# Seven-for-eight products applied twice to the queries and keys of a decoder layer, over eight tiles at once, with each half of the tokens taken through all heads by itself

## The chip, the cores and the metric

The kernel runs on one core of a Trainium2 chip. The metric is the device time of one execution in microseconds (us); less is better. The kernel before takes 1988.46 us, the median of three runs (1988.45, 1988.46 and 1991.81).

The engines of a core each work through their own list of instructions in order: TensorE (PE, matrix products, with its weight loads listed apart as PEld), VectorE (DVE), ScalarE (ACT), GpSimd (POOL), and SyncE (SP), which here only issues transfers (DMA). TensorE writes its results into PSUM, from where VectorE and ScalarE read them.

## The reference

One decoder layer on 2048 tokens (32 sequences of 64) of 512 features, all in float32. Each of the three blocks takes a layer-normalised input and is added to the residual:

```python
x = x + attn(layernorm(x))                # 32 heads of 128
x = x + xattn(layernorm(x), ctx_1024)     # one head, on the transposed layout
x = x + ffn(layernorm(x))                 # top 8 of 64 experts, each a bias vector

def attn(h):
    q = rmsnorm((h @ Wq + bq).reshape(b, n, 32, 128), gq)
    k = rmsnorm((h @ Wk + bk).reshape(b, n, 32, 128), gk)
    v = (h @ Wv + bv).reshape(b, n, 32, 128)
    p = softmax(einsum('bnhd,bmhd->bhnm', q, k) / sqrt(128))
    return einsum('bhnm,bmhd->bnhd', p, v).reshape(b, n, 4096) @ Wo + bo
```

The change concerns the first block: the products `h @ Wq` and `h @ Wk` (512 x 4096 each), and the order in which heads and tokens are gone through.

## The kernel before, in words

The tokens lie in 16 tiles of 128. Four tiles make a *quad* (512 tokens, `NQUAD` = 4), two heads make a *head group* (`HG` = 2, `NHG` = 16). The attention phase runs 64 steps: for every head group, for every quad (`order`). One step projects the quad to queries, keys and values of two heads, and does the attention of earlier steps in between.

**Seven for eight.** `HeadGroup.project` treats a step's projection as a 2 x 2 block product: two blocks of tokens (even and odd tiles of the quad) and two halves of the 512 features on the left, the same two halves of features and the two heads on the right. Instead of eight block products it makes seven, of sums and differences of blocks. The left sums (`s1` to `s4`) are made once per quad in `AttentionInput.turn`, the right ones (`t1`, `t2`, `t4` and a new `b12`) once per head group in `Weights.sums`, by POOL. Each of the seven is done once for queries and keys (`wide`, L313: four matmuls with 256 columns, j = queries or keys, c = the two 128-row parts of the half) and once for values (`narrow`, L325: four matmuls with 128 columns). A matmul in float32 shows as two records in the trace.

**Accumulating in place.** The seven results are combined in PSUM where possible: `pa` takes products 1, 6, 7 and 4 one on top of the other, and after each it is read out (`p1`, `u2`, `u3`, and the last result) by VectorE before the next is added; `pb` takes 5 and 3; `pc` takes 2. So product 6 may not start before `p1` has been read, 7 not before `u2`, 4 not before `u3`. Between two `wide` products of `pa` other products are placed. The pool `ps_a` has three buffers, for `pa`, `pc` and `pb`. Values do the same in `va` and `vb` with ScalarE copies.

**The attention of earlier steps.** In the step of unit n, `turn_probabilities` transposes the probabilities of unit n-2, `scale` (L472 on POOL for keys, L474 on VectorE for queries) multiplies the inverse root mean squares of unit n-1 in, `mix` makes probabilities times values of unit n-2 (L524), `scores` the products of queries and keys of unit n-1 (L487), `statistics` the sums of squares of unit n (L443, from squares that ScalarE made, L353), `store` copies the mixed values out (L539) and sends them to the scratch tensor `mixed` in HBM, `deviations` computes the inverse roots (ScalarE: a table load and a logarithm, L456, another table load and an exponential, L457), sends 8 KB to `row` in HBM and fetches them back broadcast over all partitions (`rsb`, 1 MB), and `probabilities` starts the softmax (VectorE maximum L235 and difference L236, ScalarE exponential L237). The rest of the softmax (sum L240, reciprocal L242, POOL product L243) and the query scalings wait in a list, `waiting`; after each product `take_waiting` puts one of them on its engine.

**Order.** The order of TensorE's instructions is the program's own everywhere, that of VectorE and ScalarE during the attention phase (`manual_schedule`). POOL's and SP's lists are arranged by a scheduler when the program is built. Weights of the next head group are fetched at quad 0, their sums are made at quads 1 and 2.

**The output phase.** `plain_out` multiplies the first two tiles of `mixed` by Wo, filling TensorE while the last attention steps drain. Then `strassen_out` does seven for eight for each further pair of tiles, with right sums from `wo_sums`, and `after_attention` runs cross-attention and experts for each tile. Constants for these (`bo_b`, `xw`, `rwt`, `rb_b`, `eb_sb`) are loaded early, in `load_constants`.

## Time and profile before

| what | us |
|---|---|
| median of three runs | 1988.46 |
| the profiled execution | 1986.83 |
| its span, first to last instruction | 1985.0 |
| TensorE busy (matmuls) | 1943.9 |
| VectorE / ScalarE / POOL busy | 963.1 / 722.0 / 526.4 |
| mean granted TensorE clock | 0.994 |
| `wide` products (L313), all matmul groups together | 856.4 |
| data moved | 185.25 MB |

A group's line gives the source line, the engine, the operation, the tiles written and read, their shapes and the count; then busy time, the mean duration of one in ns, and the idle time of the engine just before such instructions with what ended it. A line of the timeline gives the start in us from the span's start, the duration, the engine, the line, the operation, the tiles, and in brackets the engine's idle time before it. Durations of matmuls overlap, since they are pipelined; the pitch from one start to the next is the time they take.

The steady part of the attention phase is periodic: `wide` product 1 of one step starts at 805.89, that of the next at 828.04 and that of the one after at 850.18, so a step takes 22.14 us.

### The profile page before, as it was taken

The page shows a single profiled execution, that of the slowest core. Times are in us where ns is not written, and L with a number is a line of the kernel's source. Part 1 is how long each engine was busy: PE and PEld are TensorE (multiplying, and loading weights), DVE is VectorE, ACT ScalarE, POOL GpSimd, SP SyncE. Part 2 cuts the span into 40 slices and gives each one's busy share as a digit, 9 for nine tenths or more (in the row PEclk, how much of TensorE's full clock was granted, in tenths as well). Part 3 has the DMA queues.
Part 4 walks back from the last instruction along what each step waited for, and adds up shares of the span by engine and source line. Part 5 has one row for each costly group of instructions (what it writes and reads, how often), then busy time and mean ns, then how long its engine had stood idle before and what let it go on. Part 6 is the DMA issues. An engine that isn't in the chain of part 4 may idle for free.

```text
span 1985.0 us, 40265 instructions
## 1 busy us (share of the span) xinstructions
PE 1943.9 (98%) x17269; PEld 1699.8 (86%) x17269; DVE 963.1 (49%) x1766; ACT 722.0 (36%) x1499; POOL 526.4 (27%) x563
## 2 busy tenths in 40 slices
PE   6899999999999999999999999999999999999997
PEld 6788888888888888888888888888888888888875
DVE  5544444444444444444444444444453455544554
ACT  2343444444444444444444443444321112221112
POOL 4333322313132221313131232211123133331320
PEclk9999999999999999999999999999999999999997
DMA  4232222312232232223232232226423321233100
GB/s 129 93 103 98 97 100 74 118 65 97 76 118 78 84 107 87 97 66 107 82 102 97 76 108 76 97 74 193 163 94 143 109 90 62 67 109 109 43 24 21
DMA packets 126785, 185.25 MB, mean 93 GB/s; under 512 B 7312, under 2 KB 107728, under 8 KB 114320
## 3 DMA queue, kind: packets, MB, share of 16 engines
q1 hardware_dynamic: 125424, 181.61, 27.0%
q8 instruction: 136, 2.23, 0.5%
q10 hardware_dynamic: 1184, 1.08, 0.2%
q14 instruction: 41, 0.34, 0.1%
HBM read 144.39 MB, written 38.27 MB: 92 GB/s over the span
## 4 chain that ended last, share of the span: by engine, by line
PE 95%; DVE 2%; issue 1%; POOL 1%; ACT 1%; DMA 0%; POOLq 0%; DVEq 0%; ACTq 0%
PE pa L313 22%; PE py L581 19%; PE va L325 11%; PE pb L313 11%; PE vb L325 8%; PE pc L313 5%; PE o L524 4%; PE s L487 3%; PE ms L443 3%; PE pt_p L227 1%; PE py_x L793 1%; PE e_x L756 1%; PE pt_x L227 1%; PE py_x L791 1%; PE pl_f L812 1%
## 5 line engine op out<-in xcount | busy, mean ns | idle before, releaser
L353 ACT ACTIVATE sq<-qk 128x512 f32<-128x512 f32 x256 | 161.8, 632 | 610.3 <-DVE qk L350 610.3
L581 PE MATMUL py<-wo,a 128*128 128x256 f32 x1152 | 262.3, 381 | 0.0
L243 POOL TENSOR_TENSOR prob<-prob,inv 128x512 f32<-128x512 f32 x64 | 66.9, 1046 | 718.0 <-DVE inv L242 718.0
L472 POOL TENSOR_TENSOR qk<-qk,rsb 128x256 f32<-128x256 f32 x256 | 182.0, 743 | 261.5 <-DMA rsb<-row 261.5
L313 PE MATMUL pa<-xc,w 128*128 128x256 f32 x1024 | 249.7, 387 | 0.0
L313 PE MATMUL pa<-xc,t 128*128 128x256 f32 x1024 | 242.5, 380 | 6.5 <-DVE u L404 6.5
L581 PEld LDWEIGHTS py<-wo,a 128*128 128x128 f32 x1152 | 214.1, 190 | 37.3 <-issue 9.0
L313 PEld LDWEIGHTS pa<-xc,w 128*128 128x128 f32 x1024 | 185.3, 191 | 46.2 <-issue 25.9
L313 PEld LDWEIGHTS pa<-xc,t 128*128 128x128 f32 x1024 | 184.8, 190 | 26.7 <-DVE u L404 6.9
L581 PE MATMUL py<-wo_t,a 128*128 128x256 f32 x608 | 140.6, 381 | 0.0
L325 PEld LDWEIGHTS va<-t,xc 128*128 128x128 f32 x1024 | 134.4, 192 | 6.6
L539 ACT ACTIVATE ot<-o,bvt 128x256 f32<-128x256 f32 x256 | 100.6, 476 | 105.4 <-PE o L524 105.4
L325 PE MATMUL vb<-w,xc 128*128 128x128 f32 x1024 | 135.1, 275 | 0.0
L325 PE MATMUL va<-w,xc 128*128 128x128 f32 x1024 | 135.1, 275 | 0.0
L325 PE MATMUL va<-t,xc 128*128 128x128 f32 x1024 | 134.9, 275 | 0.0
L325 PEld LDWEIGHTS vb<-w,xc 128*128 128x128 f32 x1024 | 129.5, 192 | 3.3
L325 PEld LDWEIGHTS va<-w,xc 128*128 128x128 f32 x1024 | 129.5, 192 | 3.3
L474 DVE SCALAR_TENSOR_TENSOR qk<-qk,gqk,rsb 128x256 f32<-128x256 f32 x256 | 127.3, 498 | 0.0
L581 PEld LDWEIGHTS py<-wo_t,a 128*128 128x128 f32 x608 | 113.0, 190 | 14.8
L313 PE MATMUL pb<-xc,t 128*128 128x256 f32 x512 | 122.1, 382 | 0.0
L313 PE MATMUL pc<-xc,w 128*128 128x256 f32 x512 | 121.1, 379 | 0.0
L313 PE MATMUL pb<-xc,w 128*128 128x256 f32 x512 | 121.0, 379 | 0.0
(165 smaller groups left out, 2806.6 us busy)
## 6 DMA issues: line engine op xcount, KB each, us to landing
rsb<-row SPq DMA_DIRECT2D x64, 1024.0 KB
mixed<-ot SPq DMA_DIRECT2D x64, 512.0 KB
a<-mixed SPq DMA_DIRECT2D x32, 1024.0 KB
x<-in_x_dram SPq DMA_DIRECT2D x32, 256.0 KB
w<-in_wq_dram SPq DMA_DIRECT2D x32, 256.0 KB
wo<-in_wo_dram SPq DMA_DIRECT2D x8, 1024.0 KB
w<-in_wk_dram SPq DMA_DIRECT2D x30, 256.0 KB
w<-in_wv_dram SPq DMA_DIRECT2D x30, 256.0 KB
```

Of the source, the lines that this page charges most:

```text
L227: nc.tensor.transpose(pt[:, j, :], src[:, j, :], ident)
L243: nc.gpsimd.tensor_tensor(prob, prob, _bc(inv, k), ALU.mult)
L313: nc.tensor.matmul(to[:, j, :], right[i][:, c, j, :], left[i][:, c, :, :].rearrange("p j n -> p (j n)"), start=first and j == 0 and c == 0 ...
L325: nc.tensor.matmul(to[:, j, :], left[i][:, c, j, :], right[i][:, c, 2, :], start=first and j == 0 and c == 0, stop=c == 1, skip_group_chec ...
L353: nc.scalar.activation(sq, it, AF.Square)
L443: nc.tensor.matmul(ms[rows, ab, :], ones, self.sq[h, ab][:, j, :], start=True, stop=True,)
L472: nc.gpsimd.tensor_tensor(k, k, self.rs[:, 2 * h + 1, ab, :], ALU.mult)
L474: lambda q=q, rs=self.rs[:, 2 * h, ab, :]: nc.vector.scalar_tensor_tensor(q, q, gqk, rs, ALU.mult, ALU.mult)
L487: nc.tensor.matmul(s[h * SEQ : (h + 1) * SEQ, i, b, :], qk[:, 0, tok], qk[:, 1, tok], start=True, stop=True,)
L524: nc.tensor.matmul(o[b][dims, h, i, :], self.v[h, i % 2][rows, i // 2, dims], probt[rows, i, h * SEQ : (h + 1) * SEQ], start=True, stop=True,)
L539: nc.scalar.activation(ot[:, h, :, b * SEQ : (b + 1) * SEQ], o[b][:, h, :, :], AF.Identity, bias=bvt[:, hg * HG + h : hg * HG + h + 1],)
L581: nc.tensor.matmul(py, a[:, g, :], b[g // KH][:, g % KH, :], start=n == 0 and g == 0, stop=n == last and g == NHG - 1,)
```

## The change

For head groups 1 to 15 two quads are now projected at once (`Window`, eight tiles, 1024 tokens). Each of the seven outer products for queries and keys has the shape (256 features) x (two quads' blocks of 256 columns) x (queries and keys), and is itself done as a 2 x 2 block product with seven instead of eight: seven matmuls of 128 x 128 weights on 256 columns. Left sums of the second level are made by `inner_inputs` once per half of the tokens, right ones by `more_sums` once per use of a head group's weights, on POOL. Values stay at one level. Head group 0 runs as before, quad by quad (`single`).

The loop order changes: all 16 head groups for the first half of the tokens, then all 16 for the second half, so each group's weights are fetched and summed twice. The steady unit is a window of one head group and two quads, of which there are 30; there are four single steps.

```diff
+        def outer(self, o, to, add=None, bias=None):
+            left, right = halves_x[self.half, o], self.w.inner[o]
...
+            def product(i, bank, first=True):
+                nc.tensor.matmul(
+                    bank, right[i], left[i], start=first, stop=True, skip_group_check=True
+                )
+
+            def read(bank, t, j, out):
+                b = None if bias is None else bqk[:, j, bias : bias + 1]
+                if add is not None and b is not None:
+                    nc.vector.scalar_tensor_tensor(
+                        out, bank, b, add[t][:, j, :], ALU.add, ALU.add
+                    )
+                elif add is not None:
+                    nc.vector.tensor_tensor(out, bank, add[t][:, j, :], ALU.add)
+                elif b is not None:
+                    nc.scalar.activation(out, bank, AF.Identity, bias=b)
+                else:
+                    nc.scalar.copy(out, bank)
...
+            pa = bank("pa")
+            product(1, pa)
+            p1 = part("p1", "p1")
+            read(pa, 0, 0, p1)
+            pc = bank("pc")
+            product(2, pc)
+            nc.vector.tensor_tensor(to[0][:, 0, :], pc, p1, ALU.add)
+            pb = bank("pb")
+            product(5, pb)
+            product(6, pa, first=False)
+            u2 = part("u2", "u2")
+            read(pa, 0, 1, u2)
+            yield
+            product(7, pa, first=False)
+            u3 = part("u3", "p1")
+            read(pa, 1, 1, u3)
+            nc.vector.tensor_tensor(to[1][:, 1, :], pb, u3, ALU.add)
+            yield
+            product(4, pa, first=False)
+            read(pa, 1, 0, to[1][:, 0, :])
+            product(3, pb, first=False)
+            nc.vector.tensor_tensor(to[0][:, 1, :], pb, u2, ALU.add)
+            take_waiting()
```

At each of the two `yield`s of an outer product, `run` puts one product of the values (`self.v()`) and then whatever is listed for that place (o, n); place (o, 2) is after the outer product:

```diff
+            c11 = tiles(0, 0)
+            run(1, c11)
+            place(1, 2)
+            c12 = tiles(1, 0)
+            run(6, c12, c11)
+            place(6, 2)
+            c21 = tiles(0, 1)
+            run(7, c21, c12)
+            place(7, 2)
+            c22 = tiles(1, 1)
+            run(5, c22, None, heads[1])
+            for t in range(2):
+                nc.gpsimd.tensor_tensor(c12[t], c12[t], c22[t], ALU.add)
+            for t in range(2):
+                nc.gpsimd.tensor_tensor(c22[t], c22[t], c21[t], ALU.add)
+            place(5, 2)
+            run(2, c11, c11, heads[0])
+            squares(1, 1)
+            squares(0, 0)
+            place(2, 2)
+            run(4, c21, c21, heads[0])
+            squares(0, 1)
+            run(3, c12, c12)
+            squares(1, 0)
+            place(3, 2)
...
+        places = {
+            (6, 1): line.turn,
+            (6, 2): line.scale,
+            (7, 2): line.scale,
+            (5, 2): line.scale,
+            (2, 2): lambda: attend(0),
+            (4, 1): line.scale,
+            (3, 1): line.turn,
+            (3, 2): end,
+        }
```

`attend` does for one unit what the end of a step did: `mix`, `scores`, the sums of squares, `store`, the inverse roots and `probabilities`, in this order; it comes twice in a window, after outer product 2 and after outer product 3, which is the window's last. The sums of squares of a window are taken in two parts, first of (head 0, even tiles) and (head 1, odd tiles), then of the other two. `Line.scale` does half of a unit's scaling at a time, four times in a window, from a fetch of 512 KB:

```diff
-            self.rs = work.tile([P, 2 * HG, 2, QT], F32, tag="rsb", name=f"rsb_{name}", bufs=1)
...
+            self.rs = work.tile(
+                [P, 2, 2, QT], F32, tag="rsb", name=f"rs{part}_{self.name}", bufs=1
+            )
```

The weights of a group and all their sums lie in one of two 32 KB blocks (`four_blocks`), the seven left blocks of a half of the tokens in a pool of seven 8 KB blocks. In the last window the loads of Wo take over these blocks (`wo_0` and `a_0` early, the second column half of Wo after the window's products), and `drain` interleaves the last attention work with `plain_out`. The constants of the output phase are now loaded after the attention phase's pool is closed:

```diff
+    bo_b = work.tile([P, D], F32, tag="bo", name="bo_b", bufs=1)
+    load(bo_b, bo.partition_broadcast(P))
+
+    xw = work.tile([P, 4, P], F32, tag="xw", name="xw", bufs=1)
+    nc.gpsimd.memset(xw, 0.0)
+    for j, src in enumerate((xwq_t, xwk_t, xwv_t, xws_t)):
+        for b in range(2):
+            half = slice(b * SEQ, (b + 1) * SEQ)
+            load(xw[half, j, half], src)
...
     pt = ps_t.tile([P, 2, P], F32, tag="pt", name="pt_xw")
     for j in range(2):
         nc.tensor.transpose(pt[:, j, :], xw[:, j, :], ident)
```

The sums of the second level, and the order of groups:

```diff
+        def more_sums(self):
...
+                nc.gpsimd.tensor_tensor(t1, b12, b11, ALU.subtract)
+                nc.gpsimd.tensor_tensor(t2, b22, t1, ALU.subtract)
+                nc.gpsimd.tensor_tensor(t4, b21, t2, ALU.subtract)
+                nc.gpsimd.tensor_tensor(b12, b22, b12, ALU.subtract)
...
-    order = [(hg, quad) for hg in range(NHG) for quad in range(NQUAD)]
...
+    groups = [(hg, half) for half in range(2) for hg in range(NHG)]
```

## The prediction

> **What bounds the kernel now.** First the busy shares and the chain of work that ended last:

> ```profile
> PE 1943.9 (98%) x17269; PEld 1699.8 (86%) x17269; DVE 963.1 (49%) x1766; ACT 722.0 (36%) x1499; POOL 526.4 (27%) x563
> ...
> PE 95%; DVE 2%; issue 1%; POOL 1%; ACT 1%; DMA 0%; POOLq 0%; DVEq 0%; ACTq 0%
> ```

> TensorE sets the time, and nearly nothing holds it up. So a matmul removed is worth its pitch, and a wait added is worth its length. Why TensorE never waits is seen in the timeline of one step boundary:

> ```profile
> 802.71 1.16 PE L524 MATMUL o<-probt,v 64*64 64x64 f32 x64
> 803.91 1.57 ACT L539 ACTIVATE ot<-o,bvt 128x256 f32<-128x256 f32 x4 [1.25 <-PE o L524]
> 804.89 1.07 PE L443 MATMUL ms<-sq,ones 128*32 128x256 f32 x16
> 805.89 1.99 PE L313 MATMUL pa<-xc,w 128*128 128x256 f32 x8
> 806.07 1.28 ACT L456 ACT_TABLE_LOAD   x1 [0.59 <-PE ms L443]
> 807.92 0.69 DVE L368 TENSOR_TENSOR p<-pa,bqk 128x512 f32<-128x512 f32 x1 [1.43 <-PE pa L313]
> 809.90 0.62 ACT L237 ACTIVATE prob<-prob 128x512 f32<-128x512 f32 x1
> 810.42 0.35 ACT L374 COPY v<-va 128x256 f32<-128x256 f32 x1
> 810.55 0.69 DVE L240 TENSOR_REDUCE sums<-prob 128x8 f32<-128x512 f32 x1 [1.94 <-ACT prob L237]
> 811.23 1.89 PE L313 MATMUL pa<-xc,t 128*128 128x256 f32 x8
> ```

> After `ms` ScalarE needs until 810.52, 4.63 us after TensorE went on at 805.89, for two table loads and three activations; the value copy L374 stands behind them, and VectorE waits there too (L240). TensorE doesn't notice: the next read of `pa` (L368) is VectorE's and comes first, and product 6, which needs it, starts only at 811.23, after two wide (1.73 each) and two narrow products (0.89). Third, what a late read costs:

> ```profile
> 60.70 1.99 PE L313 MATMUL pa<-xc,t 128*128 128x256 f32 x8 [3.30 <-DVE u L404]
> 62.53 1.04 PE L227 MATMUL pt_a<-ident,x 128*128 128x128 f32 x8
> ...
> 1961.05 1.09 PE L227 MATMUL pt_f<-ident,xn_f 128*128 128x128 f32 x4 [3.71 <-DVE inv_x L782]
> ```

> The read L404 ended at 60.64, the matmul began at 60.70: 0.06 us to release it. A wide product after a wait has a pitch of 1.83 instead of 1.73: 0.1 for the restart. From the groups, the durations for the new shapes:

> ```profile
> L361 DVE TENSOR_TENSOR v<-vb,w 128x256 f32<-128x256 f32 x128 | 54.3, 424 | 74.0 <-PE vb L325 42.1 <-ACT w L413 31.6
> L395 ACT COPY w<-va 128x256 f32<-128x256 f32 x64 | 23.9, 373 | 85.0 <-PE va L325 85.0
> L125 POOL TENSOR_TENSOR t<-w,t 128x768 f32<-128x768 f32 x31 | 56.5, 1822 | 5.5 <-DMA w<-in_wv_dram 5.4
> ```

> **What goes.** A window replaces two steps (44.28 us). Its queries and keys take 49 matmuls of 256 columns instead of 56; a wide product of four takes 1.73, so one takes 0.432, and seven are 3.02 us per window. Values, mix, scores, sums of squares and transposes keep their counts. Over 30 windows 91 us: the whole possible gain.

> **What covers shrink.** A product on `pa` is now one matmul, 0.432, not four. A reader starts 0.20 us after the pitch of its product ends (L368: 807.92 against 807.72), takes 0.36 (ScalarE) or 0.42 (VectorE), and releases after 0.06. I follow one window:

> *First outer product after `attend(1)`.* It adds nothing and has no bias, so its reads are ScalarE copies, and in ScalarE's order they stand behind `store`, both table loads and the exponential. Read 0.36 and 0.05 more after 4.63, release 0.06: product 6 at 5.10 after `ms`; products 1, 2 and 5 cover 1.30. Wait 3.8. I take 3.4, because `ms` itself ends 0.45 later (below) while ScalarE's chain, which starts with `store`, moves less. Bounds 2.9 and 3.8. Behind the waiting copy on ScalarE stand the reads for `u2`, `u3` and the value copies, and TensorE behind all of them.

> *First outer product after `attend(0)`* (outer 4). Here VectorE reads, but `take_waiting` puts the softmax sum between `u2` and `u3`, and it waits for the exponential: 4.63 + 0.03 + 0.92 (sum and reciprocal) + 0.47 (read with two additions, by L474's 498 ns and L361's 424) + 0.06 = 6.11; product 4 is due after 4 x 0.432 + 0.89 + 0.432 + 0.89 = 3.94. That is 2.2; 1.9 with `ms` late. Bounds 1.2 and 3.0.

> *Sums of squares.* After outer 2 ScalarE has four squares (632 ns each), after outer 3 two, where before one was left; `store` follows them, and `ms` waits for the PSUM buffer that the first half of `store` frees (the same three buffers go round). Squares of (1,1) also need POOL's two additions of `c22`. I get 0.8 and 0.5, together 1.3; bounds 0.5 and 1.6.

> *From one outer product to the next.* Product 1 reuses `pa`, read last after product 4; only product 3 covers: 0.20 + 0.42 + 0.06 - 0.43 = 0.25, up to 0.43 where a query scaling (0.48) or the copy `probt` (0.69) is ahead in VectorE's queue. Five of these, with small waits for `u3` and the value copies, 2.0. Bounds 1.0 (if a read of 256 takes half of 512's 692) and 3.0.

> *Restarts.* Some 13 waits per window, 0.1 each: 1.3; bounds 0.8 and 1.5.

> Sum per window: -3.02 + 3.4 + 1.9 + 1.3 + 2.0 + 1.3 = +6.9, so 51.2 instead of 44.28; 30 windows +207. The bounds together give +3.4 to +9.9.

> **What I cost at nothing, and its cover.** POOL per window, in us: four sums of 768 (1.82), sums and additions of 512 (eight, 1.25, between L243's 1046 ns and the 1308 of the residual sum) and 384 (four, 1.0, between 743 at 256 and 1046), eight scalings (0.73), two products (1.04): 29 of 51. If its queue slipped by 3 us the squares would slip with it. VectorE gets 41 operations at 0.42 for 14 at 0.69: +7.5, some 29 of 51. The weights fetched twice add 25 MB; SP issues six transfers of about 0.47 us at the window's start, 1.57 MB at the 350 GB/s seen in the stretch of the Wo loads are 4.5 us, and the sums have until the window's end. The inverse roots come in four fetches of 512 KB, each only when POOL and VectorE have used the one before: in the rows 1 MB took 4.7 us from issue (811.83) to use (816.51), of which 3 are the data, so 3.2 here; outer products are five to six apart, which covers it. At 4.7 the query scaling would block VectorE in outers 5 and 2: +1.8 per window.

> **The clock.** The gap at the window's start is as long as the gaps at which rows begin to differ: after 3.30 the clock stayed (granted 1.00 there), after 3.71 it fell (0.51 from 1960 to 1970). A cold restart costs about 1.0 (the wide product at 29.65 took 2.90 for 1.89). I take a fall in five windows, +5 us; bounds 0 and 30. [...]

> **Once.** In the drain VectorE's list has four Wo sums ahead of the softmax end that `pt_p` needs after one chunk of `plain_out`. They wait for four loads of 1 MB that can start only as the last window frees its blocks, about 2 us before its products end: 1 + 4 x 3.0 + 1.5 (a fetch between) later, then 2.3 for the last sum, 2 for sum, reciprocal and POOL: TensorE is ready at 5.6 after the products, the probabilities at 18: 12 us; bounds 0 and 15. At the start of `strassen_out` the transposes of `xw` wait for its memset, which POOL has behind two sums of 2048 (4.52 each), then for SP's 11 issues and a 1 MB load of `a12`: 8.5; bounds 0 and 15. The second half's first inputs are turned with only `attend` as cover: 2. The four single steps otherwise cost what the first four cost before. Together 23.

> Against the profiled execution: 1986.8 + 207 + 5 + 23 = 2222. The runs' median is 1.6 above that execution, within what can be told.

> **Rivals.** *The waits are covered* and the removed matmuls come out: 1986.8 - 91 + 23 = 1919. The place is product 6 of a window's first outer product; it decides whether its ScalarE read is done 1.30 us after `ms`, or all waits sum to under 3.02. For it: VectorE and ScalarE are under half busy. Against it: L374 at 810.42 shows a copy queued behind the exponential. 3%. *Shorter waits*: reads of 256 near 0.35, `store` not pushed back: +3.4 per window, 1986.8 + 102 + 10 = 2099. For it: the reads of 512 take 0.61 in pitch. 15%. *Late fetches and a cold clock*: +1.8 for late inverse roots and a fall in every window, 1986.8 + 30 x 8.7 + 30 + 23 = 2301. For it: fetches share the queue with the weights, and rows of a fetch during the Wo loads show `row` taking 2.8 instead of 1.8 us. Against it: three of the four fetches come after the weights are in. 12%. My forecast has 70%, 2150 to 2270 by itself.

> The range, 2105 to 2300, leaves out the first rival and the ends of the others. About 4 us (0.2%) is what a measurement can tell from no change. Faster 3%, same 1%, slower 96%.

> **What would show it.** Windows of about 51 us; TensorE waiting 3 to 4 us at product 6 of outer product 1, once per window, for ScalarE; 1 to 3 us in outer 4 for VectorE's `u3`; many waits of 0.2 to 0.4 on the reads of `pa`. Matmuls of 256 columns fewer by 420 records. Wrong would be: windows at 41 to 43 us, or waits mostly for POOL or transfers, or a slow clock throughout.

## The result and the profile after

| | before | after |
|---|---|---|
| median of four runs, us | 1988.45 | 2329.30 |
| lowest and highest, us | 1987.30, 1991.81 | 2323.36, 2341.39 |
| profiled execution, us | 1986.83 | 2323.36 |

The changed kernel takes 1.172 times as long, 95% interval 1.167 to 1.177. The direction was as forecast; the time, 2329, lies 29 us above the upper end of the range. The profiled executions differ by 336.5 us where the forecast had 235.

The page of the changed kernel, busy shares and chain of waits:

```profile
PE 1989.6 (86%) x16849; PEld 1652.8 (71%) x16849; DVE 1271.8 (55%) x2604; ACT 815.9 (35%) x1739; POOL 1099.7 (47%) x1015
...
PE 50%; DVE 17%; ACT 16%; DMA 10%; POOL 3%; issue 3%; SPq 0%; ACTq 0%; POOLq 0%; DVEq 0%
```

The 420 matmul records are gone (17269 to 16849), so the change does what it says. TensorE's share of the chain fell from 95% to 50%; VectorE, ScalarE and transfers have the rest. Here is what TensorE waited for in all (total, times, longest):

```profile
PE pa_w L622 <- ACT p_w L637: 100.5, 30, 3.5
PE pa_w L622 <- DVE u_w L629: 92.3, 58, 3.1
PE pt_a L234 <- DVE x L272: 23.7, 4, 12.9
PE ms_w L720 <- ACT ot L577: 21.7, 56, 0.6
PE pa L414 <- DVE u L461: 14.3, 3, 11.0
PE pa_w L622 <- DVE u_w L633: 13.1, 26, 0.9
PE pb_w L622 <- DVE qk L658: 12.8, 26, 1.3
PE pt_p L234 <- POOL prob L250: 8.4, 1, 8.4
```

The first line is product 6 behind ScalarE, once in each of the 30 windows, 3.35 us on average; the second is `u3` behind VectorE, twice in a window (53.3 us in outer product 4 and 39.0 in outer product 2). Both stand in a window's timeline, here from the last `ms` of one window on:

```profile
1059.19 1.07 PE L720 MATMUL ms_w<-sq,ones 128*32 128x256 f32 x16 [0.32 <-ACT ot L577]
1060.19 0.70 PE L622 MATMUL pa_w<-x,w 128*128 128x256 f32 x2
1060.37 1.28 ACT L589 ACT_TABLE_LOAD   x1 [0.50 <-PE ms_w L720]
1061.15 0.59 PE L622 MATMUL pb_w<-x,w 128*128 128x256 f32 x2
1064.20 0.61 ACT L244 ACTIVATE prob<-prob 128x512 f32<-128x512 f32 x1
1064.72 0.35 ACT L637 COPY p_w<-pa_w 128x256 f32<-128x256 f32 x1
1065.12 1.22 PE L622 MATMUL pa_w<-x,w 128*128 128x256 f32 x2 [3.37 <-ACT p_w L637]
1066.14 1.91 PE L353 MATMUL va<-w,x 128*128 128x128 f32 x8
1067.84 1.06 PE L622 MATMUL pa_w<-x,w 128*128 128x256 f32 x2
1068.70 1.91 PE L353 MATMUL vb<-w,x 128*128 128x128 f32 x8
1070.40 0.99 PE L622 MATMUL pa_w<-x,w 128*128 128x256 f32 x2
```

(Each single product has two records here, `x2`: 840 products on `pa_w` and 1680 records.) The copy of `p1` comes last on ScalarE, at 1064.72, and TensorE stands from 1061.75 to 1065.12. Behind the gap it is slow: a value product takes 1.91 where it takes 1.05 elsewhere, a single product 1.06 for 0.60. Such rows follow 26 of the 30 gaps.

The time from this product 6 to that of the next window is 53.2 us in the first half of the tokens and 53.3 in the second (14 periods from 960.34 to 1707.07 are 746.7), where two steps took 44.28 and the forecast had 51.2. So the windows cost 30 x 9.0 = 270 us, and some 66 us lie outside them.

### The profile page after: what moved, and what is told of

It reads as the page before. It is cut to its first block, busy times and chain, and to the rows that moved or that the text cites. A ratio compares the mean times of both kernels' runs of the same rounds, so it can differ in the third digit from the quotient of the medians.

```text
span 2321.6 us, 41752 instructions
## 1 busy us (share of the span) xinstructions
PE 1989.6 (86%) x16849; PEld 1652.8 (71%) x16849; DVE 1271.8 (55%) x2604; ACT 815.9 (35%) x1739; POOL 1099.7 (47%) x1015
## 4 chain that ended last, share of the span: by engine, by line
PE 50%; DVE 17%; ACT 16%; DMA 10%; POOL 3%; issue 3%; SPq 0%; ACTq 0%; POOLq 0%; DVEq 0%
PE py L767 16%; PE pa_w L622 10%; DMA rs<-row_w 8%; PE va L353 6%; DVE qk L512 6%; PE pb_w L622 4%; ACT L589 3%; PE vb L353 3%; ACT L590 3%; PE ms_w L720 3%; PE pc_w L622 2%; ACT ot L577 2%; DVE qk L658 2%; ACT sq L325 2%; ACT rs_w L589 2%
## 5 line engine op out<-in xcount | busy, mean ns | idle before, releaser
L622 PE MATMUL pa_w<-x,w 128*128 128x256 f32 x1680 | 547.1, 409 | 210.0 <-ACT p_w L637 100.5
L622 PEld LDWEIGHTS pa_w<-x,w 128*128 128x128 f32 x1680 | 283.7, 199 | 297.2 <-ACT p_w L637 112.6
L510 POOL TENSOR_TENSOR qk<-qk,rs 128x256 f32<-128x256 f32 x256 | 196.5, 788 | 499.6 <-DMA rs<-row_w 481.8
L353 PEld LDWEIGHTS va<-w,x 128*128 128x128 f32 x2048 | 286.3, 204 | 28.2 <-ACT w L394 14.5
L353 PE MATMUL va<-w,x 128*128 128x128 f32 x2048 | 293.4, 290 | 2.4 <-ACT w L394 0.4
L120 POOL TENSOR_TENSOR w<-w 128x768 f32<-128x768 f32 x126 | 225.9, 1815 | 111.0 <-DMA w<-in_wv_dram 105.7
L622 PE MATMUL pb_w<-x,w 128*128 128x256 f32 x840 | 256.0, 386 | 14.0 <-DVE qk L658 12.8
L325 ACT ACTIVATE sq<-qk 128x512 f32<-128x512 f32 x256 | 147.8, 623 | 287.8 <-DVE qk L663 205.3
L353 PEld LDWEIGHTS vb<-w,x 128*128 128x128 f32 x1536 | 219.0, 206 | 12.6
L353 PE MATMUL vb<-w,x 128*128 128x128 f32 x1536 | 218.3, 289 | 0.0
L512 DVE SCALAR_TENSOR_TENSOR qk<-qk,gqk,rs 128x256 f32<-128x256 f32 x256 | 189.2, 741 | 25.1 <-DMA rs<-row_w 22.6
L633 DVE TENSOR_TENSOR u_w<-pa_w,qk 128x256 f32<-128x256 f32 x180 | 76.1, 423 | 72.9 <-PE pa_w L622 72.9
```

Of the source, the lines that this page charges most:

```text
L120: on.tensor_tensor(*(it.rearrange("p c j d -> p (c j) d") for it in (out, a, b)), ALU.subtract)
L325: nc.scalar.activation(sq, of, AF.Square)
L353: nc.tensor.matmul(to[:, j, :], left[i][:, c, j, :], right[i][:, c, 2, :], start=first and j == 0 and c == 0, stop=c == 1, skip_group_chec ...
L510: nc.gpsimd.tensor_tensor(k, k, rk, ALU.mult)
L512: lambda q=q, rq=rq: nc.vector.scalar_tensor_tensor(q, q, gqk, rq, ALU.mult, ALU.mult)
L622: nc.tensor.matmul(bank, right[i], left[i], start=first, stop=True, skip_group_check=True)
```

## Experiments

Each kernel is the changed one with the edit shown; times are medians and are set against 2329. The kernel before, run beside them, had 1990.6 to 1993.3, so differences under about 10 us are not read.

**First outer product read on VectorE**

```
-                    nc.scalar.copy(out, bank)
+                    nc.vector.tensor_copy(out, bank)
```

> The first outer product of a window is read on VectorE instead of ScalarE; nothing else. Theory (ScalarE's queue): product 6's wait of 3.37 us per window goes, because its operand no longer stands behind store, two table loads and the exponential; VectorE's softmax sum then holds u3 as in outer product 4 (1.77 us), so 1.6 us per window come back, 48 us, and another 1.2 us per window, 36 us, if the matmuls after that gap were slow because of it: about 2245 us. Rival (the wait only moves: ScalarE's value copies behind the same chain stop TensorE just as long): 2310 to 2330 us.

Measured 2234.5 us, 95 less (ratio to before 1.122, interval 1.120 to 1.124). TensorE's waits in this run:

```profile
PE pa_w L622 <- DVE u_w L629: 97.6, 58, 3.0
PE pa_w L622 <- DVE u_w L637: 48.8, 29, 1.7
PE ms_w L720 <- ACT ot L577: 22.8, 55, 2.3
```

ScalarE's line is gone; in its place `u3` of the first outer product (L637) waits 1.7 us for the softmax sum ahead of it in VectorE's list, as it does in outer product 4. The theory holds, the part about the matmuls behind the gap included: 48 us alone would have given 2281. TensorE's busy time falls from 1989.6 to 1938.4 us for the same 16849 records.

**The gap filled with matmuls**

```
             product(5, pb)
+            if o == 1:
+                for _ in range(7):
+                    product(5, pb)
             product(6, pa, first=False)
```

> In the first outer product of each window product 5 is computed eight times instead of once (same operands, same place), 7 x 0.43 = 3.0 us of matmuls in the gap before product 6, which can start no earlier than before; the wait left is 0.4 us. Theory (the idle gap makes the clock fall): the matmuls after the gap take 0.43 us again, 1.0 to 1.5 us less per window, 30 to 45 us in all, 2285 to 2300 us, and the granted clock of the windows is near 1.00. Rival (those matmuls are slow for another reason, or the clock falls for another reason): 2325 to 2335 us.

Measured 2282.6 us, 47 less (1.146, interval 1.143 to 1.148) with 210 matmuls more. Two stretches, first of the changed kernel and then of this run (busy time of TensorE, its weight loads, VectorE, ScalarE, POOL; then the granted clock, the DMA share and GB/s):

```profile
200.00:400.00 200.00, 170.99 (x1714) 141.45 (x1712) 116.33 (x249) 85.00 (x159) 107.36 (x98) 0.97 0.29 92
1200.00:1400.00 200.00, 169.70 (x1686) 141.30 (x1686) 111.27 (x239) 85.42 (x159) 103.71 (x93) 0.94 0.28 91
```

```profile
200.00:400.00 200.00, 178.10 (x1776) 148.11 (x1777) 119.16 (x250) 89.04 (x166) 109.73 (x100) 1.00 0.30 96
1200.00:1400.00 200.00, 177.32 (x1691) 148.00 (x1690) 121.02 (x255) 83.27 (x158) 114.44 (x101) 1.00 0.27 85
```

Product 6 can start no earlier, yet each window is 1.6 us shorter by the medians (1.2 to 1.4 in the two profiled executions): the clock stays at 1.00. So the idle gap of 3.4 us is followed by a lower clock in nearly every window (26 of the 30 of the changed kernel), which costs 1.2 to 1.6 us beside the gap itself.

**Softmax end one place later, and the softmax's exponential first**

```
             next(it)
+            waiting.append(lambda: None)
             waiting.append(lambda: next(it, None))
```

> The softmax sum, reciprocal and normalization are taken by VectorE and POOL one place later, behind u3 and its addition. Theory (VectorE's list): the wait of 1.77 us for u3 in outer product 4 goes, 30 x 1.77 = 53 us, about 2277 us; in the first outer product the wait for ScalarE stays. Rival (it is only pushed on: product 4 waits for its read behind the same sum, or the transposes of the probabilities wait for POOL): 2315 to 2340 us.

Measured 2320.6 us, 9 less (1.165, interval 1.163 to 1.167), which is too little to read. The waits for `u3` do fall, from 92.3 to 37.7 us. In the last stage one group's probabilities are turned before they are normalized here. The rival: product 2 of the next outer product now waits, 32.0 us in 30 times, for the read that stands behind the sum. A second edit takes the cause away instead:

```
-            if deviations:
-                deviations()
             if self.before:
                 self.before.probabilities()
+            if deviations:
+                deviations()
```

> In attend the softmax's exponential is put ahead of the logarithm and exponential of the inverse roots on ScalarE, with both table loads behind it; nothing else. Theory (the softmax sum in VectorE's list waits for an exponential that is third in ScalarE's chain): the exponential is done some 2.5 us sooner, u3 in outer product 4 no longer waits, 30 x 1.77 = 53 us less, about 2276 us; product 6 of the first outer product still waits 3.4 us, since its read stands behind the same chain. Rival (as in the run before, the wait is pushed on to the next read): 2310 to 2330 us.

Measured 2283.7 us, 46 less (1.147, interval 1.143 to 1.151):

```profile
PE pa_w L622 <- ACT p_w L637: 105.6, 30, 3.6
PE pa_w L622 <- DVE u_w L629: 37.8, 28, 2.9
```

Of the 58 waits for `u3`, those of outer product 4 are gone and the 28 of outer product 2 stay; ScalarE's are 5 us longer. What was late was the exponential, third in ScalarE's chain.

**Two fetches of inverse roots for one**

```
-            self.rs = work.tile(... tag="rsb", bufs=1)
-            nc.sync.dma_start(out=self.rs ..., in_=self.row[part] ...)
+            for h in range(HG):
+                rs = work.tile([P, 2, QT], F32, tag=f"rsb{h}", ...)
+                nc.sync.dma_start(out=rs, in_=self.row[part][:, h, :].partition_broadcast(P))
```

> Each fetch of inverse roots, 512 KB for two heads, becomes two of 256 KB into buffers of their own, so that the first head's starts as soon as its scalings are done. Theory (VectorE's query scaling waits for the fetch and holds u3 in outer product 2, 1.4 us per window): half to all of it goes, 25 to 45 us, 2285 to 2305 us. Rival (VectorE is late there for its own work, the fetch is hidden): 2325 to 2335 us.

Measured 2282.0 us, 47 less (1.145, interval 1.143 to 1.147); the waits for `u3` of outer products 4 and 2 (L629 before the edit) fall from 92.3 to 68.3 us, all of it in outer product 2 (39.0 to 15.0), and the waits for `pb` in outer product 5 (12.8) are gone. That is just above the theory's upper end. So the time of the fetch decides most of this wait, though POOL's work is the same; how it does so is seen next.

**What TensorE waits for in outer product 2.** The changed kernel's timeline there:

```profile
1036.08 2.48 POOL L702 TENSOR_TENSOR qk<-qk,qk 128x512 f32<-128x512 f32 x2
1037.32 1.53 DVE L512 SCALAR_TENSOR_TENSOR qk<-qk,gqk,rs 128x256 f32<-128x256 f32 x1 [0.25 <-DMA rs<-row_w]
1038.77 0.47 DVE L629 SCALAR_TENSOR_TENSOR u_w<-pa_w,bqk,qk 128x256 f32<-128x256 f32 x1
1039.30 0.70 PE L622 MATMUL pa_w<-x,w 128*128 128x256 f32 x2 [1.44 <-DVE u_w L629]
```

The query scaling waits 0.25 us for its fetch and then takes 1.53 us, where it mostly took 0.48 before; `u3` stands behind it. All its records between 200 and 700 us, parted by whether a POOL instruction ran at its start or began within 0.06 us of it:

| us on VectorE | alone | beside POOL, mean (longest) |
|---|---|---|
| query scaling, before (L474) | 0.48 (74 records) | 0.57 (0.97), 17 records |
| query scaling, after (L512) | 0.48 (20) | 0.87 (1.52), 58 |
| read of `pa` with an addition, after (L633) | 0.42 (42) | 0.42 (0.43), 71 |

The scaling reads two operands from SBUF; L633 reads one from PSUM and is not touched. How long a scaling lasts follows from POOL: of the 110 in this trace that start with more than 0.25 us of a POOL instruction still to run, every one ends 0.27 to 0.30 us behind that instruction. Over the 30 windows VectorE is idle for the fetch 0.44 us on average ahead of the scaling in outer product 2, the scaling takes 1.22 and TensorE waits 1.30. With two fetches it was 0.01, 0.92 and 0.50: a scaling that starts sooner finds less of POOL's work beside it. Three runs were to show what this is worth.

```
-                waiting.append(lambda ...: nc.vector.scalar_tensor_tensor(q, q, gqk, rq, ...))
+                nc.gpsimd.tensor_tensor(q, q, rq, ALU.mult)
```

> The changed kernel with the scaling of the queries on POOL, behind that of the keys, instead of on VectorE; the common gain of queries and keys is left out. Theory (VectorE's query scalings, which wait for the fetch and are stretched while POOL works, 0.87 us on average against 0.48 with POOL idle, hold u3 in outer products 2 and 5): those waits, 1.4 and 0.45 us per window, and some restarts go, 50 to 65 us less: about 2270 us, although POOL has 5.9 us more to do per window. Rival (POOL's list is what is late; more work there makes it later): 2330 to 2370 us.

Measured 2572.8 us, 244 more (1.291, interval 1.288 to 1.293):

```profile
PE ms_w L716 <- ACT ot L573: 331.0, 57, 14.9
PE pa_w L618 <- ACT p_w L633: 101.4, 30, 3.5
...
PE pa_w L618 <- DVE u_w L625: 19.2, 23, 1.8
```

The waits for `u3` do go (92.3 to 19.2), but the rival is right in kind, and its 2330 to 2370 far too low: POOL's four scalings now wait for each fetch, the sums of `c12` and `c22` stand behind them, the squares behind those, and `ms` waits 11 us per window. POOL is busy 49% of the span only; it is the order in its list that counts.

```
-                nc.gpsimd.tensor_tensor(t1, b12, b11, ALU.subtract)
...
+                    4: r[:, 1, 0, :],
+                    5: r[:, 0, 1, :],
+                    6: r[:, 1, 1, :],
```

> The changed kernel without the second-level sums of the weights (eight subtractions on POOL per window, 9 us); the products of the second level read first-level parts in their place, so matmuls keep count and shape. Theory (POOL's work stretches VectorE's scalings and delays the fetches behind its own): 15 to 35 us less, 2295 to 2315 us, and the scalings in outer product 5 take 0.5 us. Rival (POOL is covered, as the forecast had it): 2325 to 2332 us.

Measured 2266.3 us, 63 less (1.137, interval 1.134 to 1.140), twice what was expected: the waits at L633 (13.1 us; this is outer product 7, the expectations call it 5) are gone and those at the kernel's start are shorter (23.7 to 15.5, 14.3 to 6.5), but outer product 2 still waits 1.3 us on average, since the pair sums run there, not these. The other half of the 63 us is no wait at all: for the same 16849 records TensorE is busy 32 us less, at a granted clock of 0.976 for 0.956. The gap before product 6 is as long as ever (3.38 us), but here it is followed by a fall of the clock in 14 windows, in the changed kernel in 26; the last section shows on what that hangs.

```
-            for t in range(2):
-                nc.gpsimd.tensor_tensor(c12[t], c12[t], c22[t], ALU.add)
-            for t in range(2):
-                nc.gpsimd.tensor_tensor(c22[t], c22[t], c21[t], ALU.add)
```

> The changed kernel without POOL's four additions on the queries and keys behind outer product 5 (5.0 us per window); nothing takes their place. Theory (VectorE's query scaling in outer product 2 takes 1.53 us instead of 0.48 because POOL works on these at the same time): it takes 0.5 us, the wait of 1.44 us for u3 shrinks to 0.3 or less, 30 x 1.2 to 1.5 = 36 to 45 us less, 2285 to 2293 us. Rival (the fetch alone is late): the scaling starts no sooner and takes as long, 2320 to 2332 us.

Measured 2300.0 us, 29 less (1.155, interval 1.151 to 1.160), between theory and rival. Outer product 2 in this run:

```profile
1021.54 1.05 DVE L512 SCALAR_TENSOR_TENSOR qk<-qk,gqk,rs 128x256 f32<-128x256 f32 x1 [0.21 <-DMA rs<-row_w]
1021.58 1.60 POOL L510 TENSOR_TENSOR qk<-qk,rs 128x256 f32<-128x256 f32 x2 [3.90 <-DMA rs<-row_w]
1023.04 0.70 PE L622 MATMUL pa_w<-x,w 128*128 128x256 f32 x2 [0.92 <-DVE u_w L629]
```

In these two windows the fetch is as late (0.21 for 0.25), the scaling takes 1.05 instead of 1.53 and the wait is 0.92 instead of 1.44. Over the 30 windows the scaling takes 1.02 for 1.22, and the wait falls by less, from 39.0 to 32.7 us in all. The scaling does not come down to 0.48, since POOL's key scaling starts on the same fetch 0.04 us later and overlaps it. So of 1.30 us on average 0.44 are the late fetch and 0.74 the overlap with POOL, and an earlier fetch takes more out of both than POOL's additions do.

The 29 us of this run, too, are only in part waits. In the profiled executions:

| | span, us | TensorE busy | not busy | granted clock | gaps before product 6 with a fall of the clock behind |
|---|---|---|---|---|---|
| changed kernel | 2321.6 | 1989.6 | 332.0 | 0.956 | 26 of 30 |
| two fetches | 2274.8 | 1978.2 | 296.6 | 0.961 | 28 |
| no second-level sums | 2260.4 | 1957.2 | 303.2 | 0.976 | 14 |
| no pair sums | 2295.6 | 1973.2 | 322.4 | 0.966 | 22 |

All four have 16849 records, so busy time differs by the clock and the rest of the span by waits.

**One level only.** The halves, the second fetch of the weights and the order of the stages stay; every step is a single one.

```
-            double(Window(units, w, half), between, last)
+            single(units[0], None)
...
+            single(units[1], None, (hg, half) == (NHG - 1, 0))
```

> Each half of the tokens goes through all heads by itself, with the weights fetched twice, but every step is a single one with seven-for-eight products applied once, as before; no second-level inputs or sums. Theory (halves and second fetches cost only at the start, in the middle and at the end): steps of 22.14 us as before, and one-time waits of 50 to 70 us: 2035 to 2060 us, so that some 270 us of the loss belong to the windows. Rival (the second fetch or the halves slow every step): above 2080 us.

Measured 2026.0 us, 34 more than before (1.018, interval 1.016 to 1.020). Its largest waits:

```profile
PE pt_a L234 <- DVE x L272: 13.4, 4, 9.8
PE pt_p L234 <- POOL prob L250: 11.7, 1, 11.7
PE py L767 <- DMA a<-mixed: 7.7, 1, 7.7
PE pa L414 <- DVE u L461: 7.3, 4, 4.4
```

All are single waits at the start, in the middle and at the end. So 303 of the 341 us belong to the windows with their second level.

**POOL in program order where a half begins**

```
         if hg == 0:
+            with tc.manual_schedule(engines={mybir.EngineType.Pool}):
                 single(units[0], True)
```

> In the two head groups that begin a half, POOL's instructions stand in the order in which the program names them, so that the sums of the next group's weights come behind the layer norms of the inputs; nothing else. Theory (POOL's list holds up the inverse deviations, and with them VectorE's normalization and TensorE's transposes): the waits of 12.9 and 7.3 us at the start and 11.0 us in the middle shrink to about 5, 0 and 2 us, 20 to 24 us less: about 2306 us. Rival (these transposes wait for the inputs' loads): 2325 to 2332 us.

Measured 2303.6 us, 26 less (1.158, interval 1.155 to 1.160); the waits for `pt_a` fall from 23.7 to 7.1 us and those for `pa` L414 from 14.3 to 5.0. POOL had put the sums for the next head group ahead of the layer norm's deviations.

**Together.** Reads on VectorE, exponential first, two fetches and POOL in order in one kernel:

> Four edits together: first outer product read on VectorE, two fetches of inverse roots, softmax's exponential first, POOL in program order in the two groups that begin a half. Theory (each wait has its own cause): 2329 - 95 - 47 - 2 x 1.75 x 30 - 22 = 2060 us, windows of about 45 us. Rival (the waits share VectorE's queue, so removing one lets another grow): 2110 to 2180 us. Neither theory has it faster than before.

Measured 2107.9 us, 221 less (1.059, interval 1.057 to 1.061), between theory and rival: windows of 46.4 us. The edits alone gave 95 + 46 + 47 + 26 = 214, and the second softmax end should have added some 50. What is left, and one row of the second half's first window:

```profile
PE pa_w L620 <- DVE u_w L627: 27.4, 28, 3.5
PE pa_w L620 <- DVE u_w L631: 25.4, 25, 8.8
PE ms_w L718 <- ACT ot L575: 20.2, 57, 1.7
```

```profile
850.76 9.23 DVE L510 SCALAR_TENSOR_TENSOR qk<-qk,gqk,rs 128x256 f32<-128x256 f32 x1
850.96 2.24 POOL L151 TENSOR_TENSOR w<-w 128x512 f32<-128x512 f32 x2
...
858.68 1.02 POOL L153 TENSOR_TENSOR w<-w 128x384 f32<-128x384 f32 x1
859.91 0.41 DVE L631 TENSOR_TENSOR u_w<-pa_w,qk 128x256 f32<-128x256 f32 x1
```

Here one scaling lasts 9.23 us, beside eight POOL subtractions without a pause, until 0.29 us after the last has ended.

**Scalings and roots moved, on top of the four edits.** In two runs the scalings were taken two places later, and in the second of them the inverse roots too:

```
+            waiting.extend([lambda: None] * (2 if later else 0))
             for h in range(HG):
```

> The four edits together, and in the windows VectorE's query scalings taken two places later, behind u3 and its addition. Theory (they hold u3 in outer products 2 and 5, 0.67 and 0.95 us in the run with four edits): 30 x (1.62 + 0.2 for two restarts) = 55 us less than that run, about 2053 us, windows of 44.6 us instead of 46.4. Rival (a scaling that is blocked holds whatever read comes next): 2095 to 2110 us.

> As the run before, and the logarithm and exponential of the inverse roots are issued on ScalarE later, behind the second value product of the next outer product instead of directly behind the softmax's exponential. Theory (the value copies behind that chain hold VectorE's value sums, and these the reads of pa, 0.45 and 0.42 us per window): 25 to 30 us less than the run before, about 2027 us, still slower than the kernel before by some 40 us. Rival (the chain then holds the next value copies just as long): no change to the run before.

Measured 2310.7 (1.160, interval 1.158 to 1.162) and 2319.0 us (1.164, interval 1.161 to 1.167). Inconclusive: the places add up in the list, so that some queries are scaled only behind their scores and the softmax end slips too; TensorE waits 138 and 153 us at the turning of the probabilities. Done without that, both scalings at the end of an outer product, and then with the roots later, and with POOL in order only in a half's first step:

```
+            if later:
+                waiting.extend([lambda: None] * 2)
+                waiting.append(lambda: [it() for it in queries])
```

> The four edits together, and in the windows both query scalings of a fetch taken by VectorE at the end of an outer product, behind its last read, instead of one ahead of u3 and one behind it. Theory (a scaling that is stretched while POOL works, or waits for its fetch, holds u3 in outer products 2 and 5): 30 x (0.67 + 0.95 + 0.2 for restarts) = 55 us less than the run with four edits, about 2053 us. Rival (it then holds the first read of the next outer product as long): 2095 to 2110 us.

> As the run before, and the logarithm and exponential of the inverse roots issued on ScalarE behind the second value product of the next outer product. Theory (value copies behind that chain hold VectorE's value sums and with them reads of pa, 0.45 and 0.42 us per window): 25 us less than the run before. Rival: they hold the next value copies as long, no change. A version faster than before, 1990 us, is not expected of either.

> As the run before, with POOL in program order only in the first step of each half instead of the first two. Theory (in the second step the order puts second-level sums ahead of key scalings, and a scaling on VectorE stood 9.2 us beside them in the first window of the second half): the single waits of 8.8, 3.9 and 3.8 us go or halve, 8 to 15 us less. Rival (the scheduler puts the sums ahead of the layer norms again): 10 to 20 us more.

Measured 2143.4 (1.076, interval 1.074 to 1.077), 2162.5 (1.085, interval 1.081 to 1.089) and 2186.6 us (1.097, interval 1.095 to 1.099): 36 more than the four edits, then 19 and 24 more again. All three theories fall. The waits for `u3` are gone, but the pair of scalings, 1.4 to 3.0 us, now stands ahead of the next `p1` (40.5 us in 29 waits) and ahead of the softmax's maximum, and `ms` waits 57.0 us where it waited 20.2. No place in VectorE's list tried here is free of them, and no version run reaches the kernel before.

## Why the prediction was wrong

By its own steps, in the order of the sum:

- *What goes*, -3.02 per window: as forecast, 420 records.
- *Product 6 of the first outer product*, 3.4: measured 3.37 in the steady windows. The mechanism is shown by the reads on VectorE and the size is right.
- *Outer product 4*, 1.9: measured 1.77; shown by the exponential put first.
- *Sums of squares*, 1.3: 0.32 and 0.46, together 0.8. The squares were ready sooner; only `store` held `ms`.
- *Hand-over and restarts*, 3.3: in the window from 1007.31 to 1060.19 (52.88 us) 11.62 are over 41.26. The named waits (3.38, 1.77, 0.78, 1.44) take 7.4 of it, the clock 1.6 if the filled gap's mean is taken, and 2.7 remain. Only a size, 0.6 too large.
- *What I cost at nothing* failed, in two sentences. That "outer products are five to six apart, which covers it" did not hold for the fetches: in outer product 2 VectorE stands idle for one in 28 of 30 windows. And "VectorE gets 41 operations at 0.42" did not ask at what price they run beside POOL, whose busy time went from 526 to 1100 us: the query scaling went from 498 to 741 ns on average, and to 1.22 us in outer product 2. TensorE waits 1.30 us there, 0.44 in outer product 5 and 0.44 in 7. I had a price for this very wait, 1.8 per window "at 4.7", and set it aside; outer products 2 and 5 measured 1.74. But the price was for a late fetch alone, and most of the time is the overlap with POOL that the late fetch brings about. The rows show what the overlap does: 0.48 alone, up to 1.52 beside POOL with an end 0.28 behind POOL's instruction, 0.42 either way for the read of `pa` (L633). A start ahead of POOL does not always spare the scaling: 31 of the changed kernel started 0.04 us ahead of POOL's key scaling and still took 1.05, while one that started 0.11 ahead took 0.48 and the key scaling 0.96 for 0.73. By what the two engines hold each other up is not shown. The forecast had not looked for any of it.
- *The clock* failed: "I take a fall in five windows, +5 us". Filling the gap gave 47 us, with a granted clock of 1.00 in place of 0.94 to 0.97. The upper bound and the rival have a fall in every window, 30 us, which no run shows; 26 of the 30 gaps had a fall behind them, so these 30 us were nearer than my 5. My own rows (3.30 kept, 3.71 fell) left 3.4 between, and I took the kinder side. The length of the gap was the wrong thing to read; the last section shows the better one.
- *Once*, 23: about 66. The run with one level puts 34 on the halves themselves; POOL's order at the start of a half, which I had not read, was worth 26, though not all of it on top of the 34: the waits for `pt_a` and `pa` L414, 38.0 us in the changed kernel, are 20.7 in that run and were 17.0 in the kernel before. "The four single steps otherwise cost what the first four cost before" was the wrong sentence: their layer norms stand behind the second-level sums in POOL's list. The drain's wait was 8.4 for 12 (the terms as written add up to 18.8, which makes it 13), the output stage's 9.9 in all for 8.5.

In the windows 270 - 212 = 58 us were missed: clock +42, the scaling in outer product 2 +39, sums of squares -16, outer product 4 -4, hand-overs -18, which makes 43. The 15 left are not parted; the small waits in outer products 7 and 5 (13 us each), which change from window to window, may hold part of them. Outside the windows it is 66 - 23 = 43. The rival "late fetches and a cold clock", 2301, came nearest; it had the clock right, and the right wait with part of its cause. Its closeness is partly luck: it left out the 43 us outside the windows.

The expected 91 us were not lost to one thing. Each window saves 3.0 us of matmuls and loses 12.0 to waits that the old steps covered and to the slower clock behind the longest of them.

## What to carry to other kernels

Splitting a product into many small dependent ones saves matmuls but takes the cover from every read-back: count, for each accumulator, what runs between a read's release and its next use, and what stands ahead of that read in its engine's in-order list. Moving one read or swapping two calls was worth 46 to 95 us here, while each second-level matmul saved was worth 0.43. An engine at half load was not a free engine here (POOL was busy 47% of the span, and VectorE's query scaling took 0.87 us on average beside it for 0.48 alone): look at which of another engine's instructions it stretches, and at what its list puts first.

## What the runs showed of the hardware

```profile
84.74:88.15 3.41, 0.90 (x4) 1.00 0.00 0
88.15:91.56 3.41, 3.41 (x14) 0.50 0.65 207
955.14:958.55 3.41, 1.83 (x14) 1.00 0.92 235
958.55:961.97 3.42, 1.63 (x11) 1.00 0.98 299
961.97:965.38 3.41, 3.41 (x21) 1.00 0.38 132
```

The gap of 2.51 us before 87.92 lies in one stretch, and the clock falls; the gap of 3.37 before 960.34 is cut into 1.58 and 1.79, and it stays. So do the other three (at 567, 779 and 1442 us), and the gap of 3.30 in the kernel before (1.59 and 1.71). In the changed kernel all 38 falls follow a stretch with 2.02 us idle or more, and none of the 575 stretches with 1.97 or less is followed by one; in the kernel before all 3 falls follow a stretch with 2.12 or more, and none of the 566 with 1.87 or less is followed by one. So with gaps of 3.4 us it hung on their place on the grid, which no edit here chose, how many windows paid.

- Seven redundant matmuls in an idle gap, 210 in all, made the kernel 47 us faster.
